# Two graph attention layers on one core: stores issued ahead of fetches, and divisions, block transposes, a bias and a turned input moved within the step

## The chip, the cores and the metric

The kernel runs on one core of a Trainium2 chip. The metric is the device time of one execution in microseconds; lower is better. Five engines run their own instruction queues side by side: TensorE (PE in the profile; PEld are its weight loads), VectorE (DVE), ScalarE (ACT), GpSimd (POOL) and SyncE (SP). In this kernel all DMAs are issued from SP's queue.

## The reference, cut to what matters

The input is `x`, 128 batches of 128 rows of 512 values, and `adj`, a 128 x 128 mask for each batch. Two layers follow, each an attention over the rows of a batch, restricted by the mask, with a residual and a layer norm:

```python
# layer 0: 4 heads of 64
q, k, v = split_heads(x @ Wq), split_heads(x @ Wk), split_heads(x @ Wv)
sim  = where(adj, q k^T / 8, -max)
x    = layernorm(x + softmax(sim) v @ Wo + bo)
# layer 1: 8 heads of 64, layer norm ahead of the projections, mask with the diagonal
h       = layernorm(x) * gamma + beta
q, k, v = split(h @ w_qkv.T)
scores  = where(adj | eye, q k^T / 8, -1e9)
x       = layernorm(x + softmax(scores) v @ w_out.T + b_out)
```

All arithmetic is in float32.

## The kernel before, in words

**Groups and steps.** Two batches make a group, so there are 64 groups. The program is a software pipeline written out by hand: `step(s)` holds pieces of several groups at different stages. In step `s`, layer 0 attention scores and softmax work on group s-1, layer 0's output projection on group s-2, layer 1's q, k and v on group s-3, layer 1's scores and softmax on group s-4 and its output projection on group s-5; layer 0's q, k and v are made for group s. `opening()` fills the pipeline, `step` runs for s = 2 to 63, `closing` for s = 64 to 66, and `last` empties it. The schedule is manual: every engine executes its instructions in the order in which the functions are called, and a call issues instructions on several engines at once. So a line that moves in `step` moves on every queue that it touches.

**Three softmax parts.** Part 0 is layer 0 (two batches of 4 heads), parts 1 and 2 are the two batches of layer 1 (8 heads each). For a part, `scores` makes 8 blocks of 128 x 128 in PSUM; `masked` copies the allowed entries over a tile `sm` that `cleared` has filled with a large negative number (L551 on POOL, L565 on DVE); `maxima` takes negated row maxima `nmax` (L571, DVE); `exps` runs 4 exponentials per half on ACT, each with a read of its row sum (L580); `normalised` takes the reciprocal of the sums `rec` (L588, DVE) and multiplies the tile by it (L589, POOL); `blocks` transposes it in 32 x 32 blocks on DVE into `turnedp` (L604) and stores that to DRAM (L214, SP); `probs_arrive` fetches it back in four pieces (L220, SP) in the order that completes the transpose; `attend` multiplies with v on PE (L650) and ACT copies the result to `aT`.

**Turned inputs.** In the same way `turn` transposes a group's rows in blocks on DVE (L229) and stores them (layer 0's from `x`, layer 1's from the normalised `R`), and `arrive` fetches them back. `in_order` and `finish` (ACT) bring them into the tile `xT`.

**Products with 7 multiplications.** Every projection is done by a scheme of Strassen's kind, with products numbered 1 to 7: four operand sums are made on POOL (`xs`, `so`, L302), and the products accumulate in three PSUM banks a, c and f, some of which are read between two accumulations. `product_0` is layer 0's q, k and v, `qk` and `v` are layer 1's, `out_product` is the output projection of either layer. In bank a the products 1, 6, 7 and 4 follow one another. For the output projection, DVE adds the bank to the residual row `r` after every product (L502), and the next product may not overwrite the bank before that add has read it. For `product_0` ACT evicts 1, 6 and 5 to tiles `e` (L469), DVE adds after 2, 7 and 3 (L474), and ACT copies 4 (L471).

**Layer 1's q and k.** After each `qk` product DVE adds and block-transposes (L374, L381) into `tk` and `tq`; `taken_tokens` issues the stores of both from SP (L384, L386), `k_arrive` and `q_arrive` the fetches, and `q_in_order` scales q into `qo` on ACT (L412). The scores of layer 1 (`sc_a`, `sc_f`, L536) read `qo` and the fetched `kt`.

**Residual and norm.** `addend(1, g)` scales the residual row on ACT (L670) and adds the bias on POOL (L671); `addend(0, g)` adds only. `stats` runs the batch-norm statistics on DVE (L682, L683), then `roots` on POOL computes the root and the shift. The normalisation itself (L716, ACT, and for layer 1 the store of the output) waits in the list `later` until the next `flush()`; `latest` holds a small computation on POOL in the same manner.

Of the kernel before, what the change touches and what calls it, by code (L numbers as in the profile page):

```python
# [27 lines left out]
def kernel(ctx: ExitStack, tc: tile.TileContext, x, adj, wq, wk, wv, wo, bo,  # L28
# [28 lines left out]
    def flush(what=later):  # L57
        while what:
            what.pop(0)()
# [173 lines left out]
    def arrive(l, g):  # L233
        if not 0 <= g < NG:
            return
        RAW[l] = one.tile([P, 4, G, KC, 32], F32, tag=("raw0", "raw")[l], name=f"raw{l}_{g}")
        fetch(RAW[l].rearrange("p a b c i -> p a (b c i)"), SCR[l])
# [336 lines left out]
    def exps(s, part, *halves):  # L574
        if group_of(s, part) is None:
            return
        sm, nmax, total = SM[part], NMAX[part], TOTAL[part]
        for i in halves:
            for k in range(K1):
                nc.scalar.activation(sm[:, i, k, :], sm[:, i, k, :], AF.Exp, bias=nmax[:, i, k:k + 1],  # L580
                                     accum_out=total[:, i, k:k + 1])
# [179 lines left out]
    def v(g, *which):  # L761
        for i in which:
            product("v", g, i)
# [47 lines left out]
    def step(s):  # L811

        made = scores(s)
        load_ahead(s + 1)
        if s > 2:
            in_order(s)
            sums(0, s)
        arrive(1, s - 3)
        masked(made, s, 0, 1, 2)
        attend(s)  # L820
        maxima(s, 0, 1)
        out_sums(0, s - 2)
        exps(s, 0, 0)
        product_0(s, 1)
        exps(s, 0, 1)
        out_product(0, s - 2, 1, 2, 5)
        maxima(s, 2)
        product_0(s, 2)
        flush()
        load_rows(s - 1)  # L830
        normalised(s, 0)
        out_product(0, s - 2, 6, 3)
        exps(s, 1, 0)
        stats(0, s - 2, 0)
        product_0(s, 6)
        exps(s, 1, 1)
        finish(s - 3, 0)
        out_product(0, s - 2, 7)
        product_0(s, 5)
        out_product(0, s - 2, 4)  # L840
        stats(0, s - 2, 1)
        exps(s, 2, 0)
        product_0(s, 7)
        finish(s - 3, 1)
        normalised(s, 1)
        product_0(s, 3)
        blocks(s, 0)
        turn(0, s + 1)
        exps(s, 2, 1)
        product_0(s, 4)  # L850
        if s in (2, 3):
            prepare(len(setup) - (s == 2))
        blocks(s, 1)
        probs_arrive(s, 0)
        qk(s - 3, 1)
        if s == 2:
            weight_sums(w1qk, wsqk, 1)
            prepare(1)
        flush()
        arrive(0, s + 1)  # L860
        qk(s - 3, 2)
        normalised(s, 2)
        probs_arrive(s, 1)
        qk(s - 3, 6, 5)
        flush(latest)
        turn(1, s - 2)
        qk(s - 3, 7)
        k_arrive(s - 3, 0)
        cleared(s + 1, 0, 1)
        out_sums(1, s - 5)  # L870
        qk(s - 3, 3, 4)
        blocks(s, 2)
        out_product(1, s - 5, 1, 2)
        q_arrive(s - 3)
        v(s - 3, 1, 2)
        k_arrive(s - 3, 1)
        out_product(1, s - 5, 6)
        probs_arrive(s, 2)
        v(s - 3, 6, 5)
        out_product(1, s - 5, 5)  # L880
        v(s - 3, 7, 3)
        out_product(1, s - 5, 7)
        v(s - 3, 4)
        q_in_order(s - 3)
        cleared(s + 1, 2)
        out_product(1, s - 5, 3, 4)
        addend(0, s - 1)
        stats(1, s - 5, 0)
        stats(1, s - 5, 1)
        addend(1, s - 4)  # L890
        with_self(s - 2)
        if s == 2:
            weight_sums(w1v, wsv, 0, 1)
        if s == 3:
            weight_sums_out(1)

    def closing(s):

        made = scores(s)
        arrive(1, s - 3)  # L900
        masked(made, s, 0, 1, 2)
        attend(s)
        maxima(s, 0, 1)
        finish(s - 3, 0)
        out_sums(0, s - 2)
        exps(s, 0, 0)
        out_product(0, s - 2, 1, 2, 5)
        maxima(s, 2)
        flush()
        load_rows(s - 1)  # L910
        finish(s - 3, 1)
        qk(s - 3, 1)
        exps(s, 0, 1)
        out_product(0, s - 2, 6, 3)
        qk(s - 3, 2)
        normalised(s, 0)
        exps(s, 1, 0)
        out_product(0, s - 2, 7, 4)
        stats(0, s - 2, 0)
        stats(0, s - 2, 1)  # L920
        qk(s - 3, 6)
        exps(s, 1, 1)
        out_sums(1, s - 5)
        qk(s - 3, 5)
        normalised(s, 1)
        exps(s, 2, 0)
        blocks(s, 0)
        flush()
        qk(s - 3, 7)
        exps(s, 2, 1)  # L930
        turn(1, s - 2)
        blocks(s, 1)
        probs_arrive(s, 0)
        qk(s - 3, 3)
        normalised(s, 2)
        flush(latest)
        cleared(s + 1, 0, 1)
        qk(s - 3, 4)
        probs_arrive(s, 1)
        out_product(1, s - 5, 1, 2)  # L940
        k_arrive(s - 3, 0)
        q_arrive(s - 3)
        k_arrive(s - 3, 1)
        blocks(s, 2)
        if s < NG + 2:
            v(s - 3, 1)
        out_product(1, s - 5, 6, 5)
        if s < NG + 2:
            v(s - 3, 2, 6, 5)
        out_product(1, s - 5, 7)  # L950
        probs_arrive(s, 2)
        out_product(1, s - 5, 3, 4)
        q_in_order(s - 3)
        if s < NG + 2:
            v(s - 3, 7, 3, 4)
        stats(1, s - 5, 0)
        stats(1, s - 5, 1)
        cleared(s + 1, 2)
        addend(0, s - 1)
        addend(1, s - 4)  # L960
        with_self(s - 2)

    def last():

        s = NG + 3
        made = scores(s)
        masked(made, s, 1)
        maxima(s, 1)
        attend(s)
        flush()  # L970
        exps(s, 1, 0)
        masked(made, s, 2)
        maxima(s, 2)
        v(s - 4, 1)
        exps(s, 1, 1)
        out_product(1, s - 5, 1, 2)
        exps(s, 2, 0, 1)
        out_sums(1, s - 5)
        normalised(s, 1)
        v(s - 4, 2, 6)  # L980
        addend(1, s - 4)
        v(s - 4, 5)
        out_product(1, s - 5, 6, 5)
        whole_again()
        normalised(s, 2)
        v(s - 4, 7)
        blocks_direct(s, 1)
        v(s - 4, 3)
        out_product(1, s - 5, 7, 3)
        stats(1, s - 5, 0)  # L990
        out_product(1, s - 5, 4)
        v(s - 4, 4)
        attend(s + 1, 1)
        stats(1, s - 5, 1)
        blocks_direct(s, 2)
        flush()
        out_plain(NG - 1, 0, 0)
        attend(s + 1, 2)
        out_plain(NG - 1, 0, 1)
        norm_plain(NG - 1, 0)  # L1000
        out_plain(NG - 1, 1, 0, 1)
        norm_plain(NG - 1, 1)
# [36 lines left out]
```

## Time and profile before

| | |
|---|---|
| median of 3 runs | 2922.64 us (2920.9 to 2923.71) |
| the profiled execution's own time | 2934.17 us |
| its span | 2932.4 us |
| mean granted TensorE clock | 0.994 |
| PE busy | 2797.4 us (95%) |
| DVE busy | 1951.6 us (67%) |
| POOL busy | 1745.7 us (60%) |
| ACT busy | 1540.1 us (53%) |
| share of the 16 DMA engines | 66.6% (main queue) |

The profile is one execution, read by a hardware profiler. The page gives busy times and costly groups of instructions; the waits say which engine stood idle until which instruction of another engine (or which DMA) had ended; the timeline lists instructions in order of time. In a row of the timeline the columns are the start and the length in microseconds, the engine, the line, the operation, output and input tiles, the shape, and the number of instructions merged into the row; in brackets the idle time just before it and what ended it. SP's own waits can be asked for in the same way.

### The profile page before, as it was taken

Reading aid. Unit: us, or ns where it says so; the run is one execution under the profiler, and the core shown is the slowest. Engines: PE = TensorE matmul, PEld = TensorE weight load, DVE = VectorE, ACT = ScalarE, POOL = GpSimd, SP = SyncE. Lnnn points to the kernel's source line nnn. Section 1 sums busy time; section 2 is a strip of 40 time slices with the busy share of each in tenths; the row PEclk is TensorE's granted clock in tenths of the full one; section 3 lists DMA queues with packets and bytes.
Section 4 is the critical chain, followed back from the end, with each engine's and each line's share of the span. In section 5 each row is a group of like instructions: output and inputs, shape, how many; then the busy total and the mean of one; then the engine's idle time right before and its main releaser. Section 6 shows DMA issues by size and latency. Waiting matters only on the chain. (4 is left out here: it accounts for less than half of the span.)

```text
span 2932.4 us, 54429 instructions
## 1 busy us (share of the span) xinstructions
PE 2797.4 (95%) x18077; PEld 2180.4 (74%) x18077; DVE 1951.6 (67%) x3545; ACT 1540.1 (53%) x4871; POOL 1745.7 (60%) x2311
## 2 busy tenths in 40 slices
PE   8899999999999999999999999999999999999988
PEld 7677777777777777777777777777777777777767
DVE  6566676666666666666666667666666666676665
ACT  3455464554554654645645546546456455464554
POOL 4465666656656666566566556665665665565654
PEclk9999999999999999999999999999999999999999
DMA  5657767767677677676676676776766767767642
GB/s 175 188 172 203 215 183 209 205 181 222 187 202 211 188 208 207 183 217 195 192 221 181 203 214 187 207 210 184 217 192 192 218 188 200 216 188 202 190 145 90
DMA packets 482792, 570.94 MB, mean 195 GB/s; under 512 B 60872, under 2 KB 383440, under 8 KB 482512
## 3 DMA queue, kind: packets, MB, share of 16 engines
q1 hardware_dynamic: 482512, 567.46, 66.6%
q8 instruction: 145, 2.38, 0.4%
q14 instruction: 135, 1.11, 0.1%
HBM read 304.09 MB, written 263.19 MB: 193 GB/s over the span
## 5 line engine op out<-in xcount | busy, mean ns | idle before, releaser
L580 ACT ACTIVATE sm<-sm,nmax 128x128 f32<-128x128 f32 x1536 | 596.4, 394 | 5.3 <-DVE nmax L571 5.1
L589 POOL TENSOR_TENSOR sm<-sm,rec 128x1024 f32<-128x1024 f32 x192 | 364.0, 1896 | 285.0 <-DVE rec L588 281.8
L690 POOL TENSOR_SCALAR ve<-mv 128x2 f32<-128x2 f32 x191 | 41.4, 217 | 672.5 <-DVE mv L683 667.1
L502 DVE TENSOR_TENSOR r<-oa,r 128x256 f32<-128x256 f32 x508 | 209.8, 413 | 232.2 <-PE oa L498 174.0
L604 DVE STREAM_TRANSPOSE turnedp<-sm 128x1024 f32<-128x1024 f32 x189 | 232.1, 1228 | 180.6 <-POOL sm L589 180.5
L347 ACT COPY ev<-va 128x256 f32<-128x256 f32 x128 | 47.6, 372 | 577.8 <-PE va L338 577.8
L671 POOL TENSOR_TENSOR r<-r,bias 128x1024 f32<-128x1024 f32 x128 | 302.5, 2364 | 32.1 <-ACT r L670 31.1
L580 ACT ACTIVATION_READ_ACCUMULATOR sm<-sm,nmax 128x1 f32 x1536 | 295.2, 192 | 0.0
L502 DVE TENSOR_TENSOR r<-of,r 128x256 f32<-128x256 f32 x254 | 107.8, 424 | 235.4 <-PE of L498 228.2
L302 POOL TENSOR_TENSOR xs<-xT 128x256 f32<-128x256 f32 x256 | 186.7, 729 | 99.9 <-ACT xT L268 61.1
L338 PE MATMUL qka<-wsqk,xs 128*128 128x512 f32 x496 | 233.1, 592 | 0.0
L338 PE MATMUL qkf<-w,xs 128*128 128x512 f32 x496 | 233.1, 592 | 0.0
L498 PE MATMUL of<-wo,so 128*128 128x256 f32 x760 | 211.2, 387 | 16.4 <-POOL so L302 16.1
L571 DVE TENSOR_REDUCE nmax<-sm 128x8 f32<-128x1024 f32 x192 | 226.6, 1208 | 0.2
L498 PE MATMUL oa<-wso,so 128*128 128x256 f32 x760 | 206.0, 380 | 0.3 <-DVE r L502 0.3
L716 ACT ACTIVATE r<-r,shift,root 128x512 f32<-128x512 f32 x254 | 192.3, 807 | 0.4 <-POOL shift L705 0.4
L338 PEld LDWEIGHTS qkf<-w,xs 128*128 128x128 f32 x496 | 94.2, 190 | 118.6 <-issue 118.4
L338 PEld LDWEIGHTS qka<-wsqk,xs 128*128 128x128 f32 x496 | 94.2, 190 | 118.2 <-issue 103.6
L498 PEld LDWEIGHTS of<-wo,so 128*128 128x128 f32 x760 | 140.2, 190 | 54.4 <-POOL so L302 36.6
L551 POOL MEMSET sm<- 128x1024 f32 x192 | 178.9, 951 | 1.4 <-DVE turnedp L604 1.4
L682 DVE BATCH_NORM_STATS2 st<-r 128x6 f32<-128x512 f32 x254 | 173.6, 683 | 4.3
L565 DVE COPY_PREDICATED sm<-m,sc 128x512 f32<-128x512 uint8 x256 | 172.8, 730 | 4.5 <-PE sc L531 2.0
(178 smaller groups left out, 6839.0 us busy)
## 6 DMA issues: line engine op xcount, KB each, us to landing
scrp<-turnedp SPq DMA_DIRECT2D x189, 512.0 KB, 2.9
pT<-scrp SPq DMA_DIRECT2D x756, 128.0 KB, 3.7
scr<-turned SPq DMA_DIRECT2D x125, 512.0 KB, 4.6
raw<-scr SPq DMA_DIRECT2D x500, 128.0 KB, 4.3
r<-in_x_dram SPq DMA_DIRECT2D x63, 512.0 KB, 3.7
out_dram<-r SPq DMA_DIRECT2D x63, 512.0 KB, 2.8
scrk<-tk SPq DMA_DIRECT2D x124, 256.0 KB, 4.1
kt<-scrk SPq DMA_DIRECT2D x496, 64.0 KB, 3.1
```

The costliest lines, as they stand in the source:

```text
L302: nc.gpsimd.tensor_tensor(o, a0, a1, op=op)
L338: nc.tensor.matmul(o, lhsT, rhs, start=first and m == 0, stop=m == len(todo) - 1, skip_group_check=True)
L498: nc.tensor.matmul(acc, left[:, c], right[:, c], start=first and c == 0, stop=c == hk - 1, skip_group_check=True)
L502: nc.vector.tensor_add(part, acc, part)
L551: nc.gpsimd.memset(sm, NEG1 if part else NEG0)
L571: nc.vector.tensor_reduce(NMAX[part], SM[part], AX.X, ALU.max, negate=True)
L580: nc.scalar.activation(sm[:, i, k, :], sm[:, i, k, :], AF.Exp, bias=nmax[:, i, k:k + 1], accum_out=total[:, i, k:k + 1])
L589: nc.gpsimd.tensor_tensor(SM[part], SM[part], rec[:, :, :, None].to_broadcast([P, 2, K1, N]), op=ALU.mult)
L604: nc.vector.transpose(t.rearrange("p q (h r) -> p q h r", r=32), SM.pop(part).rearrange("p i k (q r) -> p q (i k) r", r=32))
L671: nc.gpsimd.tensor_tensor(R[g], R[g], (bias0, bias1)[l][:, None, :].to_broadcast([P, G, E]), op=ALU.add)
L682: nc.vector.bn_stats(st, R[g][:, b])
L716: nc.scalar.activation(R[g][:, b], R[g][:, b], AF.Identity, bias=shift[:, b:b + 1], scale=root[:, b:b + 1])
```

## The change

Nothing is computed differently, and every engine has the same number of instructions. Calls change places in `step`:

- `normalised(s, 1)` (reciprocal and multiplication of part 1) moves from behind `finish(s - 3, 1)` to right behind part 1's exponentials, ahead of `finish(s - 3, 0)` and of output products 7 and 4.
- `blocks(s, 0)` moves up from behind `product_0` 3 to behind output product 4, ahead of the second `stats`.
- `exps(s, 2, 1)` and `normalised(s, 2)` move up, and `blocks(s, 2)` follows `qk` 2 instead of `qk` 4.
- `arrive(0, s + 1)`, `k_arrive(s - 3, 0)`, `probs_arrive(s, 2)` and `turn(1, s - 2)` move down, so that on SP's queue the third block store precedes the fetches of the next group's input and of part 1, and the stores of q and of k's second half precede the first k fetch. `turn(1, s - 2)` also follows the last k transpose on DVE.
- `q_in_order(s - 3)` moves ahead of `v` product 4 and its eviction.
- `addend(1, ...)` moves from the end of a step to the middle of the next, ahead of `out_sums(1, s - 5)`, in `step`, `closing` and `last`; the memsets of `cleared` are brought together behind `out_sums`.

```diff
@@ step
         exps(s, 1, 1)
+        normalised(s, 1)
         finish(s - 3, 0)
         out_product(0, s - 2, 7)
         product_0(s, 5)
         out_product(0, s - 2, 4)
+        blocks(s, 0)
         stats(0, s - 2, 1)
         exps(s, 2, 0)
         product_0(s, 7)
         finish(s - 3, 1)
-        normalised(s, 1)
+        exps(s, 2, 1)
         product_0(s, 3)
-        blocks(s, 0)
         turn(0, s + 1)
-        exps(s, 2, 1)
+        normalised(s, 2)
         product_0(s, 4)
...
         flush()
+        qk(s - 3, 2)
+        blocks(s, 2)
         arrive(0, s + 1)
-        qk(s - 3, 2)
-        normalised(s, 2)
         probs_arrive(s, 1)
         qk(s - 3, 6, 5)
         flush(latest)
+        addend(1, s - 5)
+        out_sums(1, s - 5)
+        qk(s - 3, 7, 3, 4)
+        k_arrive(s - 3, 0)
+        probs_arrive(s, 2)
         turn(1, s - 2)
-        qk(s - 3, 7)
-        k_arrive(s - 3, 0)
-        cleared(s + 1, 0, 1)
-        out_sums(1, s - 5)
-        qk(s - 3, 3, 4)
-        blocks(s, 2)
         out_product(1, s - 5, 1, 2)
         q_arrive(s - 3)
         v(s - 3, 1, 2)
         k_arrive(s - 3, 1)
+        cleared(s + 1, 0, 1, 2)
         out_product(1, s - 5, 6)
-        probs_arrive(s, 2)
         v(s - 3, 6, 5)
...
         out_product(1, s - 5, 7)
+        q_in_order(s - 3)
         v(s - 3, 4)
-        q_in_order(s - 3)
-        cleared(s + 1, 2)
         out_product(1, s - 5, 3, 4)
         addend(0, s - 1)
         stats(1, s - 5, 0)
         stats(1, s - 5, 1)
-        addend(1, s - 4)
         with_self(s - 2)
@@ closing, last: addend(1, s - 4) at the end of closing becomes
+        addend(1, s - 5)
         out_sums(1, s - 5)
```

## The prediction

> **What bounds the kernel now.** First the page: span, and busy time of each engine (share of the span).
>
> ```profile
> span 2932.4 us, 54429 instructions
> PE 2797.4 (95%) x18077; PEld 2180.4 (74%) x18077; DVE 1951.6 (67%) x3545; ACT 1540.1 (53%) x4871; POOL 1745.7 (60%) x2311
> ```
>
> TensorE idles for only 2932.4 - 2797.4 = 135 us, some 2 us a step. The waits say what ends that idle time (total, times, longest).
>
> ```profile
> ACT qo L412 <- DMA rawq<-scrq: 186.6, 62, 6.6
> PE sc_a L536 <- ACT qo L412: 78.1, 61, 5.7
> PE of L498 <- POOL so L302: 16.1, 47, 0.7
> DVE rec L588 <- ACT sm L580: 9.8, 5, 3.3
> ```
>
> The late fetch of q holds ScalarE, and so TensorE's layer 1 scores: 78.1/61 = 1.28 us a step. The last line: a reciprocal hardly ever waits for its exponentials. Then the timeline of one step, TensorE's rows first (start, length, what, wait before it).
>
> ```profile
> 1220.69 1.16 PE L531 MATMUL sc<-qkv 64*128 64x128 f32 x16
> 1222.88 0.37 PE L536 MATMUL sc_a<-kt,qo 64*128 64x128 f32 x1 [1.03 <-ACT qo L412]
> 1227.25 1.09 PE L650 MATMUL av<-pT,v 128*64 128x128 f32 x16 [0.34 <-DVE sm L565]
> 1236.34 0.60 PE L498 MATMUL oa<-wso,aT 128*128 128x256 f32 x2
> 1238.68 1.16 PE L460 MATMUL f<-xs,w 128*128 128x128 f32 x8 [0.41 <-ACT e L469]
> 1240.12 1.06 PE L460 MATMUL a<-xT,ws 128*128 128x128 f32 x8
> ```
>
> I count from this step's first row as 0. The layer 0 output product 4 starts at 15.65, `product_0` 4 at 19.43. From there TensorE is dense up to the next step's first row at 1265.66: 25.54. Steps 6 to 63 (58 of them) run from 186.69 to 2789.43 on the timeline, 44.87 each; the fastest take 44.34. ScalarE's and VectorE's rows of the same step:
>
> ```profile
> 1228.86 0.40 ACT L580 ACTIVATE sm<-sm,nmax 128x128 f32<-128x128 f32 x1
> 1232.32 1.51 ACT L716 ACTIVATE r<-r,shift,root 128x512 f32<-128x512 f32 x2
> 1237.09 0.20 ACT L580 ACTIVATION_READ_ACCUMULATOR sm<-sm,nmax 128x1 f32 x1
> ```
> ```profile
> 1223.06 1.34 DVE L565 COPY_PREDICATED sm<-m,sc 128x512 f32<-128x512 uint8 x2
> 1226.79 2.32 DVE L571 TENSOR_REDUCE nmax<-sm 128x8 f32<-128x1024 f32 x2
> 1235.20 0.42 DVE L502 TENSOR_TENSOR r<-oa,r 128x256 f32<-128x256 f32 x1
> 1236.97 0.42 DVE L502 TENSOR_TENSOR r<-oa,r 128x256 f32<-128x256 f32 x1 [1.35 <-PE oa L498]
> 1239.13 0.19 DVE L588 RECIPROCAL rec<-total 128x8 f32<-128x8 f32 x1
> 1240.80 1.24 DVE L604 STREAM_TRANSPOSE turnedp<-sm 128x1024 f32<-128x1024 f32 x1
> ```
>
> Part 1's exponentials end at 1237.29, its reciprocal comes at 1239.13, behind everything that TensorE needs from VectorE in this stretch. The two adds at 1235.20 and 1236.97 (output products 7 and 4) run before those exponentials are over. That is what the change turns round.
>
> **The change part by part.**
>
> *Stores ahead of fetches (SP's queue).* Now the q fetch issues at 1217.76, behind the first k fetch and the third block store. Afterwards the queue holds: q store, second k store, first k fetch, fetch of part 2's blocks, layer 1's turned store, q fetch, second k fetch. The last k transpose ends at 1209.43; two four-piece fetches at 1.8 us, two stores at 0.4 and the q fetch at 1.8 put its last issue at about 1215.6 instead of 1219.5, so q lands near 1218.3 instead of 1222.2. The wait of 1.03 (mean 1.28) goes. Part 2's block fetch moves from 1221.5 to about 1212, so the 0.34 before the third attention group goes too. The second k fetch ends by 1217.5 and lands by about 1220.6, 2 us ahead of need. The third block store now stands ahead of two fetches and waits for its transpose at about 27.5; those fetches are due a step later. Free, with 10 us to spare.
>
> *`qo` ahead of v's last eviction; layer 1's bias to mid-step.* The eviction (0.37 us) waits at most until `qo` ends near 1219.6 and is read at 1225. The scaling (two L670, 1.32 us) goes where ScalarE idles 7.10 us at a stretch, the L671 add (2.36 us) where POOL idled 7.58. The layer 0 sums then start at 1224.64 instead of 1226.99, so the 16.1 us of `of` waits go. Layer 1's sums now queue behind that add; I get their second result 2.8 us before output product 6 asks. Free. The three memsets only change order among POOL work with that same slack.
>
> *Blocks of part 2, layer 1's turn.* They swap places behind the last k transpose, 1.24 against 1.25 us in front of the same add. Nothing. The second half of part 2's exponentials and its reciprocal move up too: it waits until about 21.1, and part 1's transposes stand behind it, but the next VectorE result that TensorE needs is not due before 25. Free; if it were 4 us later the k path would begin to slip.
>
> *Part 1's reciprocal ahead of output products 7 and 4: a new wait.* VectorE takes its queue in order, so the add for product 7 now stands behind a reciprocal that needs part 1's last exponential. TensorE cannot overwrite the bank for product 4 before that add has read it. From 0 (the masks start at 2.37 in each of the 58 steps, whatever `qo` does, since VectorE is solidly busy from the last layer 1 add on):
> - maxima of part 0: 6.10 + 1.21 = 7.31; first exponential 7.34, as in the fastest steps of this trace (8.17 in the step shown, where the attention copies were late).
> - to the last accumulator read of part 1: 1237.29 - 1228.86 = 8.43, giving 15.77. The 1.41 us of norms in the middle are in it.
> - hand-over 0.05, reciprocal 0.11 to the next start, add 0.42: 16.35; TensorE starts output product 4 at 16.42 with 0.07 of hand-over (rows of such hand-overs show 0.04 to 0.14).
>
> TensorE itself would be there at 1.16 + 4.83 (scores of layer 1 to `product_0` 1 in the fast steps) + 8.06 (1228.28 to 1236.34) = 14.05. So it stalls 2.4 us, where before it stood at 15.65.
>
> *Part 0's transposes ahead of the second statistics.* They now lie between the add for product 4 and the q add that frees the bank for `product_0` 4. The add for product 4 starts 0.63 after the product (1236.34 to 1236.97): 17.05; 0.34 to the transposes; 1.16 to the statistics (1240.80 to 1241.96 is one such step); 0.73 to the aggregate, 0.10 to the q add, 0.56 of it: 19.94. `product_0` 4 starts at 20.00. TensorE alone would have come at 16.42 + 0.43 + 2 x 1.34 = 19.53, so this part costs 0.47.
>
> [...]
>
> **Sum.** A step becomes 20.00 + 25.54 = 45.54 against 44.87: +0.67, times 58 steps +38.6 us. In step 4, where layer 1's attention begins, the same wait adds about 1.5; the closing has its reciprocals where they were: 0. Against the profiled execution's own 2934.17 us this is 2974. That execution lies 11.5 above the median of 2922.64. Part of that surplus are late fetches (four steps of over 46.6), which the new chain does not feel, so the median comes out between 2974 - 11.5 = 2963 and 2974. I take 2966.
>
> Bounds of the unknown: four hand-overs between 0.04 and 0.14 instead of mine are -0.1 to +0.3 a step (-6 to +17 us). An exponential chain that also has to wait for `product_0` 6's eviction adds 0.2 (the fastest steps end theirs at 15.97): +12. If the norms' 1.41 us had no row before 13.7, the chain would be shorter by at most 0.3: -17. Own range of this case: 2945 to 2990.
>
> **Rivals.**
> - *The reciprocal finds its sums ready: faster.* For it: the early fetches do free TensorE by over 1.5 us a step, and the reciprocal now waits in only 5 cases. Against it: the exponentials ahead of it are 8.43 us of ScalarE work behind a maximum that comes no earlier. It decides when the reciprocal starts before 15.15 (44.87 - 25.54 - 4.18 of chain behind it). Without that wait, the next bound is the eviction for `product_0` 5, behind the exponentials and 0.98 us of `xT`: ScalarE is done at 17.02, `product_0` 3 follows at 17.1, `product_0` 4 at 18.45, the step is 43.99. That is -0.88 x 58 = -51: 2883 on the profiled time, 2872 on the median.
> - *Stall and gains cancel.* The chain comes out 0.6 shorter, say by hand-overs hidden behind preloaded weights: 44.9 a step, 2917 to 2929. Against it: the two terms, reciprocal wait and transposes, both add to one VectorE queue.
> - *The SP part does nothing and the wait for `qo` stays.* For it: as many fetches stand ahead of the q fetch as before. But the new chain hangs on the masks, and those of layer 1 begin only at 3.60, after scores that start at 2.2 now. So it costs nothing on top: 2966 as well, and only the waits would tell.
>
> **How the numbers follow.** Slower by the chain: 0.84, inside 2945 to 2990 in about nine cases of ten. Faster: 0.11. Cancelled: 0.05. A measurement of this kernel tells 0.2% (6 us) from no change; with it the chances are faster 0.11, same 0.05, slower 0.84. The range reaches down towards the cancelled case, 2930 to 2990; all the faster case and some of the others stay out.
>
> **What would show it.** In the profile after: `rec` waiting for `sm` on ScalarE in nearly every step (some 2 to 3 us each, 120 to 180 us in all); TensorE waiting for the add `r` in front of `oa` (over 100 us) and for the q add in front of `a` (some 0.3 to 0.5 a step); the waits on `qo` and on `so` gone, q landing before the last output product; steps of 45.5 with little scatter. I am wrong if `rec` waits long and `oa` does not, if the first exponential starts before 7, or if steps are below 44.9.

## The result, and the profile after

The changed kernel takes 3039.29 us (median of 4 runs, 3037.33 to 3044.11); beside it the kernel before took 2921.77 us (4 runs, 2920.5 to 2923.71). The ratio is 1.0404, with a 95% interval of 1.0386 to 1.0422. So it is slower, as forecast, but by 117 us where 44 were forecast, and outside the range of 2930 to 2990.

The page of the kernel after, span and busy times:

```profile
span 3039.3 us, 54138 instructions
PE 2838.4 (93%) x18077; PEld 2234.4 (74%) x18077; DVE 1927.0 (63%) x3545; ACT 1543.1 (51%) x4871; POOL 1744.8 (57%) x2311
```

The same 18077 matrix products keep TensorE busy for 41 us longer than before (2838.4 against 2797.4), and its idle time grows by 66 us (200.9 against 135.0). A longer wait alone adds no busy time, so the page already says that something besides waiting has happened. The mean granted TensorE clock of this execution is 0.976; before it was 0.994.

The waits of the kernel after (total, times, longest), those that answer to the lines shown of before:

```profile
ACT qo L412 <- DMA rawq<-scrq: 350.3, 62, 7.0
DVE rec L588 <- ACT sm L580: 171.0, 65, 3.3
PE oa L498 <- DVE r L502: 146.7, 67, 3.6
PE sc_a L536 <- ACT qo L412: 6.6, 7, 4.4
PEld sc_a L536 <- ACT qo L412: 13.7, 15, 4.6
PE a L460 <- DVE qkv L474: 7.8, 31, 0.7
```

One line of the kernel before belongs beside them, its wait of the same products for the same add:

```profile
PE oa L498 <- DVE r L502: 2.6, 3, 1.5
```

The wait of the layer 1 scores on `qo` is nearly gone from TensorE (78.1 us before, 6.6 now, 13.7 on its weight loads). In its place stands the wait of output product 4 (`oa`) for VectorE's add, 146.7 us where it was 2.6, and in front of that add the reciprocal, which now waits for part 1's last exponential in nearly every step. (ScalarE waits longer for `rawq` than before, but only because it asks earlier: counted from the step's first `qk` product, `qo` starts at 24.2 now and started at 25.9 before.)

The timeline of TensorE in step 14 of the kernel after. Step 14 runs from 562.14 to 607.77, 45.63 us:

```profile
575.40 0.61 PE L460 MATMUL f<-w,xs 128*128 128x128 f32 x4
578.51 0.70 PE L498 MATMUL oa<-wso,aT 128*128 128x256 f32 x2 [2.50 <-DVE r L502]
579.04 1.05 PE L460 MATMUL a<-xs,ws 128*128 128x128 f32 x8
582.12 1.16 PE L460 MATMUL a<-xT,ws 128*128 128x128 f32 x8 [0.24 <-DVE qkv L474]
```

VectorE and ScalarE in the same stretch:

```profile
577.73 0.20 ACT L580 ACTIVATION_READ_ACCUMULATOR sm<-sm,nmax 128x1 f32 x1
```
```profile
577.96 0.20 DVE L588 RECIPROCAL rec<-total 128x8 f32<-128x8 f32 x1 [2.77 <-ACT sm L580]
578.08 0.37 DVE L502 TENSOR_TENSOR r<-oa,r 128x256 f32<-128x256 f32 x1
579.25 0.42 DVE L502 TENSOR_TENSOR r<-oa,r 128x256 f32<-128x256 f32 x1 [0.79 <-PE oa L498]
579.59 1.24 DVE L604 STREAM_TRANSPOSE turnedp<-sm 128x1024 f32<-128x1024 f32 x1
```

This is the chain of the forecast, row by row: last row sum, reciprocal, the add for product 7, output product 4, its add, part 0's transposes, and the q add that `product_0` 4 waits for. Counted from the step's first row, output product 4 starts at 578.51 - 562.14 = 16.37 (forecast 16.42), and `product_0` 4 at 19.98 (20.00).

And TensorE in the very next step, which runs from 607.77 and takes about a microsecond longer:

```profile
621.36 0.61 PE L460 MATMUL f<-w,xs 128*128 128x128 f32 x4
624.14 0.94 PE L498 MATMUL oa<-wso,aT 128*128 128x256 f32 x2 [2.17 <-DVE r L502]
624.87 1.92 PE L460 MATMUL a<-xs,ws 128*128 128x128 f32 x8
628.99 1.06 PE L460 MATMUL a<-xT,ws 128*128 128x128 f32 x8
```

Output product 4 starts at 16.37 again, and its wait is even a little shorter. But the eight products of `product_0` that took 1.05 us take 1.92 here. The windows of the kernel after, on the two steps, show why (columns: stretch and its length; busy time and count of PE, PEld, DVE, ACT, POOL; granted clock; DMA share; GB/s):

```profile
573.27:576.68 3.41, 2.74 (x23) 2.49 (x21) 1.75 (x6) 3.41 (x14) 1.90 (x1) 1.00 0.37 137
576.68:580.09 3.41, 1.58 (x12) 1.53 (x13) 1.34 (x4) 3.41 (x16) 1.85 (x1) 1.00 0.13 29
580.09:583.50 3.41, 3.17 (x29) 2.98 (x28) 3.38 (x7) 3.25 (x14) 1.60 (x6) 1.00 0.77 303
...
621.05:624.47 3.42, 1.25 (x11) 1.03 (x10) 0.49 (x2) 3.42 (x16) 0.59 (x1) 1.00 0.40 154
624.47:627.88 3.41, 3.41 (x17) 3.32 (x16) 2.46 (x5) 3.41 (x15) 1.52 (x3) 0.50 0.50 193
```

The granted clock is 0.50 from 624.47 to 627.88, and 1.00 in the other windows shown. All stretches at 0.50 in this trace begin on one fixed grid of 3.413 us, which the windows above follow; in steps 6 to 63 each lasts one window (in the start and the closing some last two). In step 14 the grid cuts the wait in two (0.67 and 1.83 us of TensorE idle in a window) and the clock stays. In step 15 one window holds all of it, 2.17 us, and the next window runs at half rate. The 58 steady steps (6 to 63) hold 31 such stretches; the kernel before holds 4, and they are in the very four steps of over 46.6 us that the forecast had put down to late fetches. Each of them follows a wait of 1.69 to 1.99 us for `qo`, so the fetches were late, but the half rate behind them was not read. The first of them, in the kernel before:

```profile
635.51:638.92 3.41, 1.72 (x26) 1.52 (x28) 3.31 (x8) 1.32 (x3) 1.10 (x3) 1.00 0.91 207
638.92:642.33 3.41, 3.41 (x35) 3.19 (x33) 2.28 (x5) 2.08 (x4) 2.57 (x3) 0.50 1.05 269
```

With that the growth of the span, 106.9 us, can be laid out:

| stretch | before | after | difference |
|---|---|---|---|
| start, up to step 6 | 186.69 | 193.71 | +7.0 |
| steps 6 to 63, mean of one | 44.875 | 46.240 | +1.365 x 58 = +79.2 |
| from step 64 to the end | 143.0 | 163.7 | +20.8 |

Of the 58 steps, 27 without a half-rate stretch take 45.63 and 31 with one take 46.77. So the 79.2 are (45.632 - 44.875) x 58 = 43.9 for the chain, and 31 x 1.14 = 35.3 for the clock. (The 44.875 has the four half-rate steps of before in it; the other 54 take 44.73 on average.) Half of a stretch of 3.41 would be 1.7 us, but the steps with one are only 1.14 longer: on average TensorE is busy 1.31 us more in them (44.36 against 43.06) and idle 0.17 less (2.41 against 2.57). Why it is not the full 1.7 was not traced.

### The profile page after: what moved, and what is told of

It reads as the page before. It is cut to its first block, busy times and chain, and to the rows that moved or that the text cites. A ratio compares the mean times of both kernels' runs of the same rounds, so it can differ in the third digit from the quotient of the medians.

```text
span 3039.3 us, 54138 instructions
## 1 busy us (share of the span) xinstructions
PE 2838.4 (93%) x18077; PEld 2234.4 (74%) x18077; DVE 1927.0 (63%) x3545; ACT 1543.1 (51%) x4871; POOL 1744.8 (57%) x2311
## 4 chain that ended last, share of the span: by engine, by line
PE 67%; ACT 17%; DVE 7%; issue 3%; SPq 2%; DMA 2%; POOL 2%; ACTq 0%; POOLq 0%; DVEq 0%
PE qka L338 14%; ACT sm L580 12%; PE oa L498 8%; PE qkf L338 7%; PE a L460 6%; PE va L338 6%; PE av L650 6%; PE qkc L338 4%; PE of L498 3%; PE vf L338 3%; ACT r L716 3%; PE f L460 2%; DVE nmax L571 2%; SPq L220 2%; PE sc L536 2%
## 5 line engine op out<-in xcount | busy, mean ns | idle before, releaser
L502 DVE TENSOR_TENSOR r<-oa,r 128x256 f32<-128x256 f32 x508 | 206.2, 406 | 152.0 <-PE oa L498 142.0
L412 ACT ACTIVATE qo<-rawq 128x512 f32<-128x512 f32 x124 | 71.3, 621 | 350.3 <-DMA rawq<-scrq 350.3
L502 DVE TENSOR_TENSOR r<-of,r 128x256 f32<-128x256 f32 x254 | 107.3, 422 | 217.7 <-PE of L498 211.1
L498 PE MATMUL oa<-wso,aT 128*128 128x256 f32 x380 | 111.5, 403 | 138.8 <-DVE r L502 138.8
L498 PE MATMUL oa<-wso,so 128*128 128x256 f32 x760 | 210.0, 386 | 12.6 <-DVE r L502 7.9
L498 PE MATMUL of<-wo,so 128*128 128x256 f32 x760 | 209.8, 386 | 0.9 <-POOL so L302 0.7
L498 PEld LDWEIGHTS oa<-wso,aT 128*128 128x128 f32 x380 | 67.7, 191 | 157.8 <-DVE r L502 151.0
```

Of the source, the lines that this page charges most:

```text
L498: nc.tensor.matmul(acc, left[:, c], right[:, c], start=first and c == 0, stop=c == hk - 1, skip_group_check=True)
L502: nc.vector.tensor_add(part, acc, part)
```

## The experiments

The kernel before took 2935.05 us on the chip of the first four runs, 2935.57 on that of the next four and 2939.04 on that of the last three; every ratio below is against the kernel before on the same chip. The changed kernel was not run again on these chips. Where a time below is set against its 3039.29 us, the two come from different chips, on which the kernel before differs by up to 17 us (2921.77 to 2939.04); the ratios and the lengths of the steps are the safer comparison.

**1. The reciprocal of part 1 back behind `finish(s - 3, 1)`.** If the forecast's wait is the whole loss, this alone turns the change into a gain.

```diff
         exps(s, 1, 1)
-        normalised(s, 1)
         finish(s - 3, 0)
...
         finish(s - 3, 1)
+        normalised(s, 1)
         exps(s, 2, 1)
```

> The changed kernel with one call put back: part 1's reciprocal and multiplication stand behind the second layer 1 turn-in of the step again, as before the change; all else stays moved. Theory W (the wait of VectorE for part 1's exponentials makes the loss, and TensorE's half-rate stretches follow from its standing still there): the wait of the add r in front of oa goes, the half-rate stretches go with it, and a step falls from 45.63 or 46.76 us to the next bound, the eviction for product_0 5, 43.99 by the prediction's second rival; with the closing's loss of 21 us still in it some 2890 to 2915 us. Theory Q (the reordered queue of SP makes the loss, since ScalarE now waits 350 us for the q fetch instead of 187): stays above 3000 us.

Measured: 3169.12 us, ratio 1.0796 (1.0761 to 1.0831). The edit that takes the new wait away makes the kernel slower still, by 130 us (by the ratios, 1.0796 against 1.0404, some 115). Its steps take 48.50 on average, and TensorE's waits say where:

```profile
PE sc_a L536 <- ACT qo L412: 196.1, 60, 4.1
...
PE oa L498 <- DVE r L502: 9.1, 5, 3.6
```

The wait for output product 4 is gone as expected (9.1 us), but the layer 1 scores now wait 196 us for `qo`. SP's queue in one step of this kernel (start, length in which the pieces are issued, line, tiles, pieces):

```profile
904.40 0.63 SPq L214 DMA_DIRECT2D scrp<-turnedp  x1
905.07 2.65 SPq L220 DMA_DIRECT2D raw<-scr  x4
907.83 1.80 SPq L220 DMA_DIRECT2D pT<-scrp  x4
909.72 0.38 SPq L386 DMA_DIRECT2D scrq<-tq  x1
910.20 0.52 SPq L384 DMA_DIRECT2D scrk<-tk  x1
910.77 3.19 SPq L220 DMA_DIRECT2D kt<-scrk  x4
914.06 1.80 SPq L220 DMA_DIRECT2D pT<-scrp  x4
915.96 0.38 SPq L214 DMA_DIRECT2D scr<-turned  x1
916.43 2.75 SPq L220 DMA_DIRECT2D rawq<-scrq  x4
```

From the store of part 1's blocks at 904.40 to the q fetch at 916.43 SP has no pause: most issues cost it about 0.48 us, some about 1 (20 issues in 12.03 us), and the q fetch goes out when everything ahead of it is out. Two things settle when that is: the time of the store, and the number of pieces between. The change raised the number by the four pieces of part 2's fetch (`pT` at 914.06, which before stood behind both q and k). With the reciprocal where it was before, part 1's blocks are stored 5.96 us behind the start of the step's first `qk` product (5.97 before, 1.85 after the change), and the first piece of the q fetch goes out at 21.9 (20.7 before, 18.2 after). ScalarE then starts `qo` at 28.05, where the next step's first row is at 24.2 and its layer 1 scores could begin at 25.2. So the early q fetch was bought by the early reciprocal, and not by the order of stores and fetches. The new waits in turn bring 56 half-rate stretches, 239 us at half clock.

**2. The wait filled with products that nobody reads.** Six products (1.34 us; twelve instructions in the profile) of operands that are on chip anyway go to an unread PSUM tile, right where TensorE would stand idle. The result of the kernel is untouched.

```diff
+    def fill(s):
+        pt = mm_tile(f"fill_{s}")
+        for c in range(KH):
+            for t in range(3):
+                nc.tensor.matmul(pt[:, t * P:(t + 1) * P], w0[:, c, 0, t], XT[0, s][:, c, :P], start=True, stop=True)
...
         product_0(s, 5)
+        fill(s)
         out_product(0, s - 2, 4)
```

> The changed kernel with useless work added: half a dozen products of the size of product_0 5 (1.34 us) into a PSUM tile that nobody reads, in each step between product_0 5 and output product 4, where TensorE stands still for 2.5 us. Theory I (a window of 3.41 us in which TensorE was idle for about 1.94 us or more is followed by one at half rate): idle time in the windows falls to 1.2 us, the half-rate stretches of the steady steps go, every step takes 45.63 us, and the run gets faster by 31 x 1.13 = 35 us, to about 3004 us, although it computes more. Theory L (half rate comes from load or from something outside the kernel): 3039 us or more, the clock stays at 0.976.

Measured: 3008.56 us, ratio 1.0249 (1.021 to 1.0288). That is 31 us less than the changed kernel's time, with more computed. The steady steps take 45.65 on average (45.62 to 46.02), and none holds a half-rate stretch. Experiment 4 below gives the comparison on the same chip: its `step` is that of the changed kernel, and its steps take 46.28 on average, with 33 stretches. The difference of 0.63 us, times 58, is 36.5. TensorE's waits, and a window of 100 us, of this kernel:

```profile
PE oa L498 <- DVE r L502: 60.9, 61, 3.6
PE a L460 <- DVE qkv L474: 15.7, 62, 0.7
```
```profile
800.00:900.00 100.00, 96.42 (x639) 76.64 (x638) 64.46 (x122) 56.81 (x187) 58.72 (x76) 1.00 0.66 193
```

The wait left is 1.0 us a step, the clock is 1.00 throughout the steady steps, and the step's length is that of the undisturbed chain: output product 4 starts when its add is done, whether TensorE idles or works until then. This settles the 35 us.

**3. The early reciprocal alone, put into the kernel before.**

```diff
         exps(s, 1, 1)
+        normalised(s, 1)
...
         finish(s - 3, 1)
-        normalised(s, 1)
         product_0(s, 3)
```

> The kernel before with this one call moved: part 1's reciprocal and multiplication right behind part 1's exponentials. Theory W: output product 4 cannot start before 16.4 us of the step, product_0 4 not before 16.4 + 3.1 = 19.5, a step takes at least 45.07 us; with the scatter of the fetches that the kernel before has, 2935 to 2960 us. TensorE stands still for less than 1.9 us at a time, so few half-rate stretches. Theory Q: the queue of SP is that of before, so no loss, 2922 us.

Measured: 2960.08 us, ratio 1.0084 (1.0053 to 1.0116), just above the upper end. Steps take 45.29 to 45.46, 45.31 on average, and the steady ones hold no half-rate stretch. This edit alone lengthens the step by 0.44 us.

**4. Layer 1's bias back at the end of `closing`.**

```diff
@@ closing, last
-        addend(1, s - 5)
         out_sums(1, s - 5)
...
         addend(0, s - 1)
+        addend(1, s - 4)
         with_self(s - 2)
@@ ahead of closing
+    addend(1, NG - 5)
```

> The changed kernel with layer 1's bias put back to the end of the step in the closing and in the last part alone (and one call of it ahead of the closing for the group in between). Theory B (the bias of layer 1 in the closing stands ahead of part 1's multiplication on POOL and holds the tail up): the time from the last step's end, 163.7 us against 143.0 before, comes back by 15 to 20 us, 3019 to 3024 us in all; steps as in the changed kernel. Rival: the tail is longer only because the pipeline enters it in another state, and the time stays at 3039 us.

Measured: 3019.24 us, ratio 1.0279 (1.0244 to 1.0314). From step 64 to the end the run takes 142.8 us, as before the change (143.0), instead of 163.7. What went wrong there is seen on POOL's timeline of the changed kernel in `closing`:

```profile
2890.91 1.90 POOL L589 TENSOR_TENSOR sm<-sm,rec 128x1024 f32<-128x1024 f32 x1 [0.16 <-DVE rec L588]
...
2897.07 2.35 POOL L671 TENSOR_TENSOR r<-r,bias 128x1024 f32<-128x1024 f32 x1 [1.46 <-ACT r L670]
...
2902.36 1.90 POOL L589 TENSOR_TENSOR sm<-sm,rec 128x1024 f32<-128x1024 f32 x1
```

The bias add waits for its scaling on ScalarE, 1.46 us, and takes 2.35 more, and part 1's multiplication stands behind it in POOL's queue. The multiplications of part 0 and part 1 start 11.45 us apart (2890.91 and 2902.36); in experiment 4 the same two start 7.67 apart. In `step` POOL has slack at that place; in `closing`, where few groups are left to overlap, that work holds up the softmax. That the end hangs on this softmax is shown by the time that comes back, not traced row by row.

**5. As experiment 1, and part 2's block fetch back behind both q and the second k fetch.** If the four pieces ahead of the q fetch are to blame, this must give the time back.

```diff
         finish(s - 3, 1)
+        normalised(s, 1)
...
         k_arrive(s - 3, 0)
-        probs_arrive(s, 2)
         turn(1, s - 2)
...
         out_product(1, s - 5, 6)
+        probs_arrive(s, 2)
         v(s - 3, 6, 5)
```

> The kernel of the first experiment (part 1's division put back) with the fetch of part 2's blocks also put back behind the q fetch and the second k fetch. In the first experiment SP issued the q fetch 21.9 us after the first qk product, against 20.7 before the change, with four more pieces ahead of it, and TensorE's layer 1 scores waited 196 us for it. Theory P (SP's queue is full from the store of part 1's blocks to the q fetch, some 0.48 us a piece, so the four pieces moved ahead of q and the late store of part 1 make that loss): q lands 1.9 us earlier, steps fall from 48.5 to about 46, few half-rate stretches, 2960 to 3010 us. Rival: the time stays above 3100 us, and something else makes the first experiment slow.

Measured: 2939.64 us, ratio 1.0016 (1.0001 to 1.0031), 230 us faster than experiment 1, and more than expected. The q fetch goes out at 19.75, `qo` starts at 25.7, steps take 44.50 and none is over 46. The scores' wait is down to this (line of the waits):

```profile
PE sc_a L536 <- ACT qo L412: 33.5, 29, 2.5
```

A further 32 us are waits for the second k fetch. So four DMA pieces in the wrong place of one queue were worth 230 us in experiment 1. There TensorE idled up to 4 us at a stretch; over steps 6 to 63 it was idle 131 us longer than here and, with 239 us at half clock against none, busy 102 us longer. Also, without the reciprocal and part 2's fetch the change gains 0.38 us a step (44.50 against 44.87), 22 us, and the closing of 163 us takes nearly all of it away.

**6. The transposes of part 0 back behind `product_0` 3.** The forecast priced their new place at 0.47 us a step.

```diff
         out_product(0, s - 2, 4)
-        blocks(s, 0)
         stats(0, s - 2, 1)
...
         product_0(s, 3)
+        blocks(s, 0)
         turn(0, s + 1)
```

> The changed kernel with part 0's block transposes put back behind product_0 3. Theory W: product_0 4 comes at 16.4 + 3.1 = 19.5 instead of 20.0, so steps at full rate take 45.05 instead of 45.63; steps with a half-rate stretch stay at 46.76, since there TensorE itself is late; about half of each, 3018 to 3030 us. Rival: the transposes are hidden, 3039 us.

Measured: 3088.96 us, ratio 1.051 (1.0474 to 1.0545): not a gain of 0.47 x 58 us, but a loss of 50 (by the ratios, 1.051 against 1.0404, some 31). Steps take 47.17 with 30 half-rate stretches, and the waits show the same thing as in experiment 1 (both lines of TensorE):

```profile
PE sc_a L536 <- ACT qo L412: 120.1, 60, 3.7
PE oa L498 <- DVE r L502: 91.4, 64, 3.6
```

On VectorE part 0's transposes now stand shortly before part 1's, with the turned input and a reciprocal between. Part 1's blocks are stored at 4.65 instead of 1.85, the q fetch goes out at 20.4 instead of 18.2, and `qo` starts at 26.6, after the scores are due. The early transposes of part 0, like the early reciprocal, pay for the q fetch.

**7. Only the first half of the step's changes** (the reciprocals, part 0's transposes and the second half of part 2's exponentials), put into the kernel before; SP's order, the turned input and the bias stay as they were.

```diff
         exps(s, 1, 1)
+        normalised(s, 1)
...
         out_product(0, s - 2, 4)
+        blocks(s, 0)
...
-        normalised(s, 1)
+        exps(s, 2, 1)
         product_0(s, 3)
-        blocks(s, 0)
         turn(0, s + 1)
-        exps(s, 2, 1)
+        normalised(s, 2)
...
         qk(s - 3, 2)
-        normalised(s, 2)
```

> The kernel before with only the first half of the change to a step: part 1's and part 2's division, part 0's transposes and part 2's exponentials moved, everything from the qk products on (SP's queue, layer 1's bias, closing) as before. Theory W and I: the chain takes 45.6 us a step; layer 1's bias still holds output product 5 until 9.7 us of the step, so TensorE's idle time falls in two pieces of less than 1.9 us and no half-rate stretch follows; tail as before: about 2934 + 58 x 0.76 = 2978 us. If half-rate stretches come with this chain whatever else is done: about 3015 us.

Measured: 2986.34 us, ratio 1.0167 (1.0147 to 1.0188), 8 us over the expectation. Steps are 45.80 to 45.83 without exception, and no window in them runs at half rate. The same chain binds as after the change, but TensorE's idle time lies in two pieces:

```profile
PE of L498 <- POOL so L302: 91.6, 60, 1.6
PE oa L498 <- DVE r L502: 55.6, 64, 1.5
```

No window of 3.413 us in the steady steps has more than 1.57 us of idle time, and the clock stays. With the whole change the first piece goes (the sums `so` are early), TensorE reaches the second 1.5 us sooner, and its idle time gathers in the one wait of 2.5 us. So the second half of the change does what it was forecast to do, and its gain is turned into a longer wait and then into half rate.

**8. Another order with the same parts.** The two adds that free TensorE's bank go ahead of part 1's second exponentials and its reciprocal goes behind the add of `product_0` 7; both k fetches and the q fetch go ahead of part 2's block fetch; `closing` as before.

```diff
         product_0(s, 6)
-        exps(s, 1, 1)
-        normalised(s, 1)
-        finish(s - 3, 0)
         out_product(0, s - 2, 7)
         product_0(s, 5)
+        exps(s, 1, 1)
+        finish(s - 3, 0)
         out_product(0, s - 2, 4)
-        blocks(s, 0)
         stats(0, s - 2, 1)
         exps(s, 2, 0)
         product_0(s, 7)
+        normalised(s, 1)
+        blocks(s, 0)
         finish(s - 3, 1)
-        exps(s, 2, 1)
         product_0(s, 3)
         turn(0, s + 1)
-        normalised(s, 2)
...
         qk(s - 3, 1)
+        exps(s, 2, 1)
...
         qk(s - 3, 2)
-        blocks(s, 2)
+        normalised(s, 2)
         arrive(0, s + 1)
         probs_arrive(s, 1)
+        blocks(s, 2)
...
         k_arrive(s - 3, 0)
+        q_arrive(s - 3)
+        k_arrive(s - 3, 1)
         probs_arrive(s, 2)
...
-        q_arrive(s - 3)
         v(s - 3, 1, 2)
-        k_arrive(s - 3, 1)
```

> A new order that uses what the runs showed: product_0 5 and its eviction stand ahead of part 1's second half of work on ScalarE, part 1's reciprocal stands behind the q add after product_0 7, so that nothing that TensorE needs waits for these exponentials; part 0's transposes behind it; q and k are fetched ahead of part 2's blocks; part 2's second exponentials follow qk 1's eviction; the closing is as before the change. By the chain of the prediction TensorE is dense from the layer 1 scores on: product_0 4 at 17.1, a step of 42.65 us at best, 2934 - 58 x 2.2 = 2806 us; with 0.5 to 1 us a step of fetches that come late, 2835 to 2865 us. Rival: SP's queue then sets the step, and the time stays at 2900 us or above.

Measured: 2796.83 us (2795.07 to 2798.43), ratio 0.9522 (0.9502 to 0.9542): faster than both kernels, and 9 us under the best that was expected. Its page, and a window of the length of one step:

```profile
span 2793.8 us, 54130 instructions
PE 2759.1 (99%) x18077; PEld 2160.3 (77%) x18077; DVE 1933.9 (69%) x3545; ACT 1534.9 (55%) x4871; POOL 1749.7 (63%) x2311
```
```profile
500.00:542.60 42.60, 42.60 (x279) 33.19 (x278) 29.68 (x55) 23.87 (x78) 27.28 (x37) 1.00 0.70 210
```

TensorE is busy for the whole step (42.60 of 42.60), steps take 42.61 to 42.67, none holds a half-rate stretch, and the waits that carried this document are down to `PE oa L498 <- DVE r L502` with 2.6 us in all. The q fetch goes out at 17.6, and `qo` starts at 22.4 and is done at 23.6, before the next step's first row at 24.2. With TensorE busy all the time, order alone has nothing left to gain in the step, as far as this profile shows.

**9 and 10. Two and three filling products instead of six** (0.45 and 0.67 us), to find how much idle time in a window goes by without half rate in the next.

```diff
-        for c in range(KH):
-            for t in range(3):
+        for c in range(1):
+            for t in range(2):      # experiment 9; three in experiment 10: range(3)
```

> The changed kernel with two useless products (0.45 us) in the wait before output product 4. The idle piece shrinks from 2.5 to 2.05 us. Theory I with its bound at about 1.9 us of idle time in a window of 3.41: windows that hold the whole piece are still followed by half rate, so about as many half-rate stretches in the steady steps as without (31), and 3035 to 3045 us.

> The same with three useless products (0.67 us): the idle piece is 1.83 us, under the bound. Theory I: hardly any half-rate stretch in the steady steps, 3004 to 3012 us, as with six products. If the clock answers to the mean load rather than to one window's idle time: in between the run with two and the run with six, nearer to the first.

Measured: 3026.01 us, ratio 1.0295 (1.0275 to 1.0316), with 16 half-rate stretches in the steady steps; and 3020.05 us, ratio 1.0275 (1.0254 to 1.0295), with 10 (two runs each). Both miss: two products already help, and three do not end it. The table sorts the windows of 3.413 us by whether the next one ran at half rate.

| kernel | stretches in steps 6 to 63 | least idle time in a window that half rate followed | most idle time in one that it did not follow |
|---|---|---|---|
| the changed kernel | 31 | 1.94 | 1.86 |
| two filling products | 16 | 1.90 | 1.77, and one of 1.95 |
| three filling products | 10 | 1.84 | 1.82 |
| six | 0 | | |

For this wait the bound lies between about 1.8 and 1.95 us of idle time in a window. A wait of 2.5 us less 0.67 leaves 1.84, which is on the bound and not clear of it, since the wait varies by a few hundredths between steps.

It is no sharp bound, and not the same everywhere. In front of the layer 1 scores less was enough: 1.69 us in the kernel before, 1.64 in experiment 11, 1.59 in experiment 6. In front of output product 4 a window of experiment 4 with 1.91 was not followed by half rate, another with 1.82 was. In the steady steps of all these kernels no full-rate window with less than 1.59 us was followed by half rate, and every one with more than 1.95 was. So idle time alone does not decide, and what else does is not shown. The windows in front of the layer 1 scores hold the products of the layer 0 scores, over 64 rows instead of 128 (`64*128` in their timeline rows); whether that matters is not shown either.

**11. The first half of experiment 8's order alone, in the changed kernel.**

```diff
-        exps(s, 1, 1)
-        normalised(s, 1)
-        finish(s - 3, 0)
         out_product(0, s - 2, 7)
         product_0(s, 5)
+        exps(s, 1, 1)
+        finish(s - 3, 0)
         out_product(0, s - 2, 4)
-        blocks(s, 0)
...
         product_0(s, 7)
+        normalised(s, 1)
+        blocks(s, 0)
         finish(s - 3, 1)
```

> The changed kernel with only the first half of a step mended: product_0 5 ahead of part 1's second exponentials on ScalarE, part 1's reciprocal and part 0's transposes behind the q add after product_0 7. SP's queue, the bias and the closing as in the change. The wait in front of oa goes. Theory P: part 1's transposes then stand behind part 2's reciprocal until 22.4 us, the store of part 1 comes 4.0 us after qk 1 instead of 1.85, q lands 2 us later against the step, and the layer 1 scores wait about 1 us for it: steps of 43.7, with the long closing 2880 to 2900 us. Rival: q is in time, steps of 42.6, 2830 us.

Measured: 2932.44 us, ratio 0.9974 (0.9963 to 0.9986). 107 us less than the change (by the ratios, 0.9974 against 1.0404, some 126), but a miss by 30 to 50. Steps take 44.44 on average where 43.7 were expected, and three of them hold a half-rate stretch. The store of part 1's blocks (4.23) and the q fetch (20.1, about 2 us later than after the change) came as worked out, and `qo` starts at 26.2; the waits of TensorE show what they cost, and one that was not foreseen:

```profile
PE sc_a L536 <- ACT qo L412: 77.0, 60, 5.9
PE qka L338 <- ACT eqk L347: 12.3, 60, 0.2
```

The second line is TensorE waiting in the `qk` products for an eviction on ScalarE, 0.2 us a step, which the changed kernel does not have. About 0.44 us a step is lost between the first `qk` product and the next scores. An eviction queued behind part 2's exponentials would explain the 0.2; that was not tried apart from the rest. Experiment 8 moves those exponentials too and has no such wait.

## Why the prediction was right in direction and wrong in size

The profiled execution took 3041.11 us where 2974 were forecast for it. Of the 67 us, 35.3 are the half-rate stretches (experiment 2), 20.8 the closing (experiment 4), 5.5 the start, and 5.3 the chain itself (45.632 instead of 45.54, times 58). So the direction came by the mechanism that was forecast and not by luck: the chain alone makes the kernel slower. Two terms of the sum failed, the price of the wait and the 0 for the closing. Take away one of the two losses and the run would still lie above 2990; take away both and it would lie inside the range.

- *"Part 1's reciprocal ahead of output products 7 and 4: a new wait": right.* First exponential at 7.36 (7.34 forecast), last exponential over at 15.79 (15.77), output product 4 at 16.37 (16.42). The wait is 2.5 us (2.4); `rec` waits 171 us in all (120 to 180), `oa` 146.7 (over 100). Experiment 3 shows this part alone: +0.44 us a step.
- *"Part 0's transposes ahead of the second statistics", 0.47 us: right on the path, and wrong as the worth of the part.* The q add ends at 19.93 (19.94), while the wait for it is shorter and rarer than forecast (0.24 us in step 14 and 7.8 us in 31 cases, instead of 0.3 to 0.5 in each). But experiment 6 lost 50 us by undoing it, since the move also makes room for part 1's transposes and so for the q fetch.
- *"reciprocal 0.11 to the next start": right to add up distances between starts.* In step 14 the row of the reciprocal is 0.20 long and the add behind it starts 0.12 after it (577.96 and 578.08). The chain counted in such distances came out right to 0.01 us at its q add.
- *"The sum": the step that failed.* It priced a wait of 2.4 us at its length. Idle time of that length on TensorE is followed, in 31 of 58 steps, by 3.41 us at half clock, 35.3 us in all. The trace of before had the same thing in four steps, and they were read as late fetches alone, "which the new chain does not feel". Looking at the granted clock in those four steps would have shown it.
- *"The closing has its reciprocals where they were: 0": wrong, 20.8 us.* The reciprocals are there, but the bias add was moved in front of a multiplication on POOL, in a stretch with little else to overlap. "Free" was argued from POOL's idle time in `step` alone, and the edit is in `closing` and `last` as well.
- *"In step 4 ... about 1.5": too small.* Step 4 grew by 4.55 (38.01 to 42.56), the start by 7.0. What it consists of was not traced further. Some of it varies between executions: in experiment 4, with the same instructions up to there, step 4 takes 40.79 and the start 191.47 instead of 193.71.
- *"Stores ahead of fetches": the right effect, the wrong cause.* `q` did come earlier and its wait went. But the queue ahead of the q fetch had become longer by four pieces, where the third rival says "as many fetches stand ahead of the q fetch as before". The forecast counted from the last k transpose to the last issue of the q fetch, 6.2 us; in one step of the changed kernel it is 7.7 (920.43 to 928.17). What the count took for granted is that SP is free when that transpose ends. After the change it is: the second k store follows the transpose by 0.03 us in every step. That is so since part 1's blocks are stored early, through the reciprocal and transposes that the prediction treated as pure loss. In experiments 1 and 6, where they are stored later, SP is still busy, the k store comes 2.2 and 1.0 us behind the transpose (medians), and the q fetch is late again. Hence also the failed expectation of experiment 1: the parts are coupled through SP's queue.
- *The rivals.* That the reciprocal finds its sums ready was excluded by its 171 us of waits. That stall and gains cancel is excluded as well: steps at full rate are 45.63. That the SP part does nothing: the wait on `qo` is nearly gone, so it was not the case, and by experiment 1 a late `qo` would not have been free either.
- *"Steps of 45.5 with little scatter": half right.* The 27 full-rate steps have it; the others fall in a second group at 46.77.

## What to carry to other kernels

Price a wait on TensorE by more than its length: if a change gathers its idle time in one piece of about 2 us per step, as here, read the granted clock window by window, because the products behind it may run at half rate (here in 31 of 58 steps; eight products took 1.92 us instead of 1.05). In an in-order queue an operation that waits for another engine belongs behind the adds that free the bound engine's buffers (experiment 11, which puts it there, has the ratio 0.9974 where the change has 1.0404), and the time of a fetch is counted from the last thing it queues behind, piece by piece (about 0.48 us each here), and not from its place among its neighbours. Check a moved call in every function that it moves in: here a move that was free in the steady steps cost 21 us in the last few.

## What the runs showed of the hardware that was not expected

- In the traces of before and after, half-rate stretches of TensorE start on a fixed grid of 3.413 us and last one window of it in the steady steps of the changed kernel. Where the grid lies against the first instruction differs from run to run (its first point comes 0.63 us after it in the trace of before and 3.24 in that of after).
- Idle time well under the length of a window was enough: the least that half rate followed was 1.94 us in the changed kernel (where 1.86 was not followed by it), 1.84 with three filling products and 1.59 in front of the layer 1 scores of experiment 6.
- Whether a wait of 2.5 us is followed by half rate depends on where the grid cuts it, so that steps with identical instructions take 45.63 or 46.77 us in one execution.
- Products that nobody reads made the steps shorter: 46.28 us on average without them (experiment 4) and 45.65 with them (experiment 2), on the same chip.
- One queue issuing four-piece fetches back to back takes some 0.48 us a piece (1.80 us from the start of the first to the end of the last of four), at times twice that. In two kernels whose store is equally late, four pieces more in front of one fetch made the difference between 2939.64 and 3169.12 us (ratios 1.0016 and 1.0796).
